# Two row blocks of table 1 made ahead of the first addition, and the edge lists of target blocks 5 to 7 made earlier

## The chip, the cores and the metric

The kernel runs on one core of one Trainium2 chip. A core has five engines that run side by side and meet only through semaphores: PE (matrix products; weight loads are shown apart as PEld), DVE (vector work), ACT (activations and copies), POOL (here: it issues the gathers) and SP (here: it issues nearly all other transfers). Sixteen DMA engines move the data of all queues. The metric is the device time of one execution in microseconds (us), the median of several runs; lower is better.

## The reference

For each of 16 batches b, with 1024 nodes and 256 features, the layer gates each edge (u, v) of a sparse adjacency matrix (well under 1% of the entries, and the diagonal):

```
pre_u = h_t @ W1[:256]            # per source node u
pre_v = h_t @ W1[256:]            # per target node v
hidden = relu(pre_u[:, :, None, :] + pre_v[:, None, :, :] + b1)
S = sigmoid(hidden @ W2 + b2)
a_t = einsum('buv,bud->bvd', S * A_a, h_t)
m_t = einsum('uv,bud->bvd', A_m, h_t) * h_t
z_t = beta1 * h_t + beta2 * (a_t @ Wa + ba) + beta3 * (m_t @ Wm + bm)
```

Both A_a and A_m are `adj`. Only pairs with an edge matter, so the kernel works on lists of edges.

## The kernel before, in words

**Tiles.** The batches form 4 groups of 4. For each group g there is a table in DRAM (`table[g]`) with one row of 8 KB per source node: 4 KB of pre_u and 4 KB of h for the 4 batches. The 1024 nodes form 8 blocks of 128. A *row block* (g, nt) is the part of table g that belongs to source block nt; it is made from hT (the transposed h of that block, 0.5 MB, in pieces of 512 bytes) by `rows`: two halves, each a product with `w_u` on PE (`half_product`, L411), a copy from PSUM by ACT into `tab` and a write into the table by SP. The h half of the row is copied from DRAM to DRAM by SP (`copy_h`, L405).

**Lists.** For each target block vt, `lists(vt)` makes the list of its edges from one 0.5 MB piece of `adj` (`key`, loaded by SP at L238): DVE finds the nonzero places (L245, L254 to L300), ACT turns them into marks (`made`, L305 to L307), PE permutes them (L315), ACT copies the outcome (`few`, L309, and L, L319) and DVE finishes with indices (L323 to L344). Lists 0 to 3 are made ahead of the main loop; lists 4 to 7 are generators whose pieces are put between the loop's work by `fill` and `piece_of`. What a generator yields says when its next piece may come: after "load" 8 steps, after "wait" 2, after "slot" or "step" 1.

**Main loop.** The work is 32 blocks (one group and one target block each) of T = 10 steps, 320 steps n. In a step POOL gathers 128 table rows for 128 edges into one of 8 slots (`fetched`, L513, about 1 MB); PE expands the target side onto the edges (`expand`, L622: pc from the marks and X); DVE adds it (`add`, L652) and gates with relu and W2 (`gate`, four operations at L659); ACT makes the sigmoid and the weights (`left`, L662, L666); PE sums into the targets (`aggregate`, L675). A slot is free for the next gather once PE has summed from it, so up to 8 gathers run ahead; the first 8 need no freed slot. At each block's end PE transposes sums (L697) and multiplies with Wa and Wm (L746), and SP writes the result (L753). `halves(k)` makes X, the target side of block k (L415, L411 with `w_v`, L472, and `low` at L474 on DVE). The last blocks go without `low`.

**Order.** No scheduler sorts this: each engine and each queue runs its instructions in the order in which the program is written. Blocks come as group 0 with vt 0 to 5, group 1 with vt 0 to 5, group 0 with 6 and 7, group 1 with 6 and 7, then groups 2 and 3. So table 1 must be whole when the gathers of block 6 (step 60) are issued, some 8 steps earlier, and list 6 is needed for block 12. Ahead of the loop a `script` of 14 strings sets the order of the start by letters: "r" is half a row block of table 0, a digit is a piece of that list, "f" issues the first 8 gathers, "w" six warming products on PE whose result nobody reads (`warm`, L553), "h" a piece of X, "k" loads the hT of row block (1,6), "m" makes the first mark and "s" scales the bias. In the loop `made_rows(n)` makes half a row block of table 1 in the steps that `plan` lists, after loading its hT some steps earlier, when a place for it is free. There are 2 places of hT beside the 8 of group 0, which come free one after another; 3 more (`MORE`) come when all lists are done, at step `LISTS`.

Of the kernel before, what the change touches and what calls it, by code (L numbers as in the profile page):

```python
# [17 lines left out]
def kernel(  # L18
# [217 lines left out]
    def lists(vt):  # L236
# [68 lines left out]
        nc.scalar.activation(mark, slot, AF.Abs, bias=span[:, 1:2])  # L305
        nc.scalar.activation(mark, mark, AF.Sign, bias=span[:, 0:1], scale=-1.0)
        nc.scalar.activation(mark, mark, AF.Relu)  # L307
        yield "step"
        nc.scalar.copy(few, mark)  # L309
        for w in range(NW):  # L310
            for h in range(2):
# [186 lines left out]

    BS = NG * NT
    EVS = 3  # L500
    ROOM, MORE, LISTS, AHEAD = 10, 3, 110, 14
    BEHIND = (5, 6, 7, 8)
    APART, minus = 24, []

# [33 lines left out]
    for i in range(COPIES):  # L538
        copy_h(turn[i], nc.sync)

    script = ("r r 0 0", "r r 1 0 0", "r r 1", "r 0 0", "r r 1", "0 2 r 1", "0 0 r r", "1 2 r 1", "v r r 2", "r 1 3",
              "h 2 1 1", "h 2 2 3", "f 2 2 2 k w h h h", "m 3 w 3 3 3 s")
    begun_rows = {}
    marks, pcs, accs, evs, hbs, LTs, lefts = {}, {}, {}, {}, {}, {}, {}

# [14 lines left out]
        nc.vector.scalar_tensor_tensor(bias_c, bias_c, be3, ba_c, ALU.mult, ALU.add)  # L560
        hT_free.append(spare_)

    m = 0
    piece = None
    parts = halves(0)
    for t, turns_ in enumerate(script):
        step = t - 100
        do(step)
        for c in turns_.split():
            if c == "r":  # L570
                k = turn[m % NT]
                if m < NT:
                    begun_rows[k] = rows(k, tabs[m])
                    next(begun_rows[k])
                go(begun_rows[k], step)
                if m > NT and m - NT + COPIES <= NT:
                    copy_h(turn[m - NT + COPIES - 1], nc.sync)
                m += 1
            elif c == "h":
                go(parts, step)  # L580
            elif c == "v":
                fetch_val(3)
                spread(b1_p, b1_b)
                next(parts)
            elif c == "f":
                for n in range(NF):
                    fetch(n)
                    if n > 2:
                        fetch_val(1)
                bias = load_rows(bm, D, "bias", nc.sync, spare[:, 1])  # L590
                ba_b = load_rows(ba, D, "ba_b", nc.sync, spare[:, 2])
                bias_c, ba_c = fixed([P, DC], "bias_c"), fixed([P, DC], "ba_c")
                nc.sync.dma_start(bias_c, bm.rearrange("(c p) -> p c", p=P))
                nc.sync.dma_start(ba_c, ba.rearrange("(c p) -> p c", p=P))
                be1 = load_rows(beta1, 1, "be1", nc.sync)
                be2 = load_rows(beta2, 1, "be2", nc.sync)
                be3 = load_rows(beta3, 1, "be3", nc.sync)
            elif c == "k":
                load_hT(turn[NT])
            elif c == "s":  # L600
                scale_bias()
            elif c == "m":
                load_mark(0)
            elif c == "w":
                warm(6)
            else:
                next(made[int(c)], None)
# [28 lines left out]
    def piece_of(r, n):  # L636
# [2 lines left out]
        if said is None:  # L639
            running.remove(r)  # L640
        else:
            r[1:] = said not in ("slot", "step"), n + {"load": 8, "wait": 2, "slot": 1, "step": 1}.get(said, 0)

    def fill(n, gap=True):
        for r in running:
# [154 lines left out]


    advance = {0: (3,), 2: (3,), 4: (3,)}
    start_list = dict(zip((7, 14, 44, 82), range(EARLY, NT)))
    at, pending = {}, []

    def plan(blocks, ns):
# [2 lines left out]
            pending.append((pieces[0], k))  # L809
            at.update((n, k) for n in pieces)  # L810

    plan(turn[NT:], ((4, 6), (9, 11), (13, 18), (19, 21), (23, 28), (29, 31), (33, 38), (39, 41)))
    for g, first in ((2, 60), (3, 140)):
        plan([(g, vt) for vt in range(NT)], ((first + 9 + 10 * i, first + 14 + 10 * i) for i in range(NT)))
    pending.extend((order.index(k) * T - T + 1, k) for k in again)
    pending.sort()
    ending = parts = piece = last = None

# [71 lines left out]
    for n in range(total - 3):  # L890
# [17 lines left out]
        if n == 0:  # L908
            for i in advance[0]:
                next(made[i], None)  # L910
            load_hT(turn[NT + 1])
            next(made[EARLY])
            w_a, w_m = load_weights(Wa, "w_a", nc.sync), load_weights(Wm, "w_m", nc.sync)
            after(10, scale_weights)
        if n == total - 6:
            hbs[BS - 1] = next(t for t in hT_free if t in flat).rearrange("p b c n -> p b (c n)")
# [174 lines left out]
```

## Time and profile before

| | us |
|---|---|
| median of 3 runs | 1029.48 |
| lowest and highest | 1023.5, 1036.24 |
| the profiled execution | 1026.43 |
| its span, first to last instruction | 1024.6 |
| mean granted clock of PE in it | 0.984 |

The page gives, for the whole span, each engine's busy time and then, in 40 slices of 25.6 us, its busy share in tenths. A row of the timeline has the start, the time, the engine and line, output and input, and in brackets how long the engine was idle before it and what ended that. SPq and POOLq rows are issues of transfers: the time there is that of the issue, not of the transfer. Rows of the DMA queues have packets, MB and the share of 16 engines' time; q0 carries the gathers that POOL issues, q1 what SP issues. A row of the windows has busy time of PE, PEld, DVE, ACT and POOL, then PE's clock, the DMA share and GB/s.

### The profile page before, as it was taken

What the parts mean: (1) busy time and instruction counts of PE and PEld (TensorE: products, weight loads), DVE (VectorE), ACT (ScalarE), POOL (GpSimd) and SP (SyncE); (2) the same over time, 40 slices, a digit from 0 to 9 for tenths busy, and PEclk for the clock granted to TensorE, in tenths of its full rate; (3) what the DMA queues carried; (4) which work ended last, traced back from release to release, by engine and by line L of the source; (5) the groups of instructions that cost most, each with busy time, mean ns of one, the idle gap of its engine ahead of it and who ended that gap; (6) DMA issues with size and microseconds to landing.
All of it is one profiled execution on the core that took longest, in us unless ns stands there. A gap on an engine that the chain in (4) does not pass through costs nothing.

```text
span 1024.6 us, 21644 instructions
## 1 busy us (share of the span) xinstructions
PE 957.0 (93%) x6408; PEld 696.9 (68%) x6408; DVE 948.3 (93%) x3302; ACT 889.0 (87%) x2754; POOL 438.2 (43%) x441
## 2 busy tenths in 40 slices
PE   7877989998899999999999999999999999999996
PEld 5744766665566766776677777777777666677663
DVE  7588969879998999998999999999999999999994
ACT  3666978978898999888999999999999999999984
POOL 3166656555337332563343333434333434444430
PEclk9988999999999999999999999999999999999998
DMA  9899999999899999999999999999999999999992
GB/s 329 300 356 383 376 340 322 351 364 343 301 342 343 396 412 387 343 365 381 411 414 411 411 406 405 412 393 414 383 413 394 383 375 365 365 370 368 377 369 70
DMA packets 128702, 375.00 MB, mean 366 GB/s; under 512 B 17616, under 2 KB 83152, under 8 KB 92368
## 3 DMA queue, kind: packets, MB, share of 16 engines
q0 software_dynamic: 48640, 296.70, 74.3%
q1 hardware_dynamic: 79312, 76.30, 22.4%
q8 instruction: 53, 0.87, 0.3%
q10 hardware_dynamic: 624, 0.52, 0.2%
q14 instruction: 73, 0.60, 0.2%
HBM read 377.53 MB, written 50.33 MB: 418 GB/s over the span
## 4 chain that ended last, share of the span: by engine, by line
PE 56%; DVE 23%; ACT 8%; issue 8%; DMA 3%; POOL 1%; another core or an unknown queue 0%; POOLq 0%; DVEq 0%
PE misc L411 16%; DVE fetched L659 11%; PE misc L746 11%; PE pc L622 10%; PE acc L675 9%; DVE fetched L652 8%; PE misc L697 4%; DMA fetched<-table,uidx 3%; ACT left L666 2%; PE misc L730 1%; DVE LT L714 1%; PE misc L415 1%; ACT ev L683 1%; ACT X L906 1%; POOL fetched L513 1%
## 5 line engine op out<-in xcount | busy, mean ns | idle before, releaser
L513 POOL DMA_INDIRECT fetched<-table,uidx x320 | 342.7, 1071 | 501.3 <-PE acc L675 353.8
L659 DVE SCALAR_TENSOR_TENSOR fetched<-fetched,w_b 128x256 f32<-128x256 f32 x1280 | 472.3, 416 | 0.0
L652 DVE TENSOR_TENSOR fetched<-fetched,pc 128x1024 f32<-128x1024 f32 x320 | 387.6, 1211 | 28.9 <-PE pc L622 10.2
L666 ACT ACTIVATE left<-left,gt 128x16 f32<-128x16 f32 x1280 | 285.8, 299 | 0.0
L622 PE MATMUL pc<-X,mark 128*128 128x512 f32 x640 | 229.8, 451 | 20.7 <-DVE fetched L652 11.9
L675 PE MATMUL acc<-fetched,left 128*32 128x256 f32 x2560 | 183.6, 388 | 4.6 <-ACT ev L683 3.1
L622 PEld LDWEIGHTS pc<-X,mark 128*128 128x128 f32 x640 | 105.0, 189 | 109.8 <-issue 59.3
L675 PEld LDWEIGHTS acc<-fetched,left 128*32 128x32 f32 x2560 | 71.8, 109 | 81.9 <-issue 23.2
L662 ACT ACTIVATE gt<-sc,b_b 128x4 f32<-128x4 f32 x320 | 96.8, 303 | 30.4 <-DVE fetched L659 22.0
L746 PE MATMUL misc<-w_a,LT 128*128 128x256 f32 x496 | 117.4, 379 | 0.7 <-ACT LT L424 0.7
L746 PE MATMUL misc<-w_m,LT 128*128 128x256 f32 x496 | 117.3, 379 | 0.0
L746 PEld LDWEIGHTS misc<-w_a,LT 128*128 128x128 f32 x496 | 93.6, 189 | 15.6 <-ACT LT L424 1.5
L630 ACT ACTIVATE left<-onehot,val 128x32 f32<-128x32 bf16 x320 | 100.1, 313 | 0.0
L411 PE MATMUL misc<-w_u,wide 128*128 128x256 f32 x384 | 92.0, 388 | 8.0 <-DMA w_u<-in_W_dram 7.3
L353 POOL DMA_INDIRECT val<-in_adjT_dram,vidx x80 | 85.0, 1063 | 33.8 <-issue 22.8
L659 DVE DVE_READ_ACCUMULATOR fetched<-fetched,w_b 128x1 f32 x1280 | 99.0, 77 | 0.0
L683 ACT COPY ev<-acc 128x512 f32<-128x512 f32 x160 | 92.3, 577 | 6.8 <-PE acc L675 2.3
L746 PEld LDWEIGHTS misc<-w_m,LT 128*128 128x128 f32 x496 | 89.5, 190 | 9.8
L697 PE MATMUL misc<-ident,ev 128*128 128x128 f32 x642 | 83.9, 275 | 11.7 <-ACT ev L683 5.8
L411 PE MATMUL misc<-w_v,wide 128*128 128x256 f32 x368 | 91.5, 394 | 0.0
L697 PEld LDWEIGHTS misc<-ident,ev 128*128 128x128 f32 x642 | 74.5, 142 | 22.4 <-ACT ev L683 6.6
L411 PEld LDWEIGHTS misc<-w_u,wide 128*128 128x128 f32 x384 | 73.6, 194 | 21.1 <-DMA w_u<-in_W_dram 7.3
(160 smaller groups left out, 980.2 us busy)
## 6 DMA issues: line engine op xcount, KB each, us to landing
table<-in_x_dram SPq DMA_DIRECT2D x32, 512.0 KB
out_dram<-z SPq DMA_DIRECT2D x62, 256.0 KB
table<-tab SPq DMA_DIRECT2D x48, 256.0 KB
wide<-in_xT_dram SPq DMA_DIRECT2D x18, 512.0 KB
fetched<-table,uidx POOLq DMA_INDIRECT x320
hT<-in_xT_dram SPq DMA_DIRECT2D x10, 512.0 KB
wide<-in_xT_dram SPq DMA_DIRECT2D x4, 1024.0 KB
table<-fetched SPq DMA_DIRECT2D x8, 512.0 KB
```

Source lines behind the costliest of these rows:

```text
L411: nc.tensor.matmul(p[:, bb * D:(bb + 1) * D], hT[:, 2 * h + bb, i, :], wt[:, i, :], start=(i == 0 and not begun), stop=(i == DC - 1), skip ...
L513: nc.gpsimd.indirect_dma_start(out=fetched[at_slot[n]], out_offset=None, in_=table[g], in_offset=bass.IndirectOffsetOnAxis(ap=uidx[:, vt * ...
L622: nc.tensor.matmul(pcs[n][:, c], marks[n // TW][:, j * P:(j + 1) * P], cuts[k][w][:, c], start=True, stop=True)
L630: nc.scalar.activation(lefts[n][:, 1::GB, :], onehot[:, vt * NW + w, j, :].unsqueeze(1).to_broadcast([P, GB // 2, V]), AF.Copy, scale=val[ ...
L652: nc.vector.tensor_tensor(t, t, pcs.pop(n), ALU.add)
L659: nc.vector.scalar_tensor_tensor(t[:, b, :], t[:, b, :], 0.0, w2_b, ALU.max, ALU.mult, accum_out=sc[:, b:b + 1])
L662: nc.scalar.activation(gt, sc, AF.Sigmoid, bias=b2_b)
L666: nc.scalar.activation(lefts[n][:, 2 * b, :], lefts[n][:, 1 + b // 2 * GB, :], AF.Copy, scale=gt[:, b:b + 1])
L675: nc.tensor.matmul(accs[i][b * 2 * V:(b + 1) * 2 * V, r, :], left[:, 2 * b - b % 2:2 * b - b % 2 + 2].rearrange("p k v -> p (k v)"), f[:, ...
L683: nc.scalar.copy(evs[i], accs.pop(i))
L697: nc.tensor.matmul(pt[:, :, FROM[j]:FROM[j] + V], evs[i][:, r, c * P:(c + 1) * P], ident, is_transpose=True, start=(j == of[0]), stop=True ...
L746: nc.tensor.matmul(pz[:, bb * D:(bb + 1) * D], LT[:, 2 * h + bb, i if bb else 1 - i, c, :], wt[:, c, :], start=(i == 1 and bb == 0 and c = ...
```

## The change

- In the script, "k" now comes right behind "f" and loads two hT places, of (1,6) and (1,7). The second group of six warming products is gone. A new letter "x" makes half a row block; four of them stand at the end of the last two strings, so (1,6) and (1,7) are made ahead of the first addition.
- Their `copy_h` moves to step 0, behind the loads of list 4's key and of w_a and w_m. The load of hT (1,7) in step 0 is gone.
- The other six row blocks of table 1 are made in steps 8 and 9, 13 and 18, 19 and 23, 28 and 29, 33 and 38, 39 and 43 (before: eight row blocks in steps 4 to 41).
- Lists 6 and 7 start in steps 27 and 40 instead of 44 and 82, and a list waits 5 steps for its load instead of 8. `LISTS` goes from 110 to 70.
- After the three ACT operations of `made` a list now pauses 2 steps ("pause") instead of 1 ("step").
- The hT of the row blocks that are needed a second time is asked for 9 steps sooner.

```
-        yield "step"
+        yield "pause"
         nc.scalar.copy(few, mark)
...
-    ROOM, MORE, LISTS, AHEAD = 10, 3, 110, 14
+    ROOM, MORE, LISTS, AHEAD = 10, 3, 70, 14
...
-              "h 2 1 1", "h 2 2 3", "f 2 2 2 k w h h h", "m 3 w 3 3 3 s")
+              "h 2 1 1", "h 2 2 3", "f k 2 2 2 w h h h x", "m 3 x 3 3 3 s x x")
...
             elif c == "k":
-                load_hT(turn[NT])
+                for k in turn[NT:NT + 2]:
+                    load_hT(k)
+                sooner = [rows(k) for k in turn[NT:NT + 2]]
+            elif c == "x":
+                if x_made % 2 == 0:
+                    next(sooner[x_made // 2])
+                go(sooner[x_made // 2], step)
+                x_made += 1
...
-            r[1:] = said not in ("slot", "step"), n + {"load": 8, "wait": 2, "slot": 1, "step": 1}.get(said, 0)
+            r[1:] = (said not in ("slot", "step", "pause"),
+                     n + {"load": 5, "wait": 2, "slot": 1, "step": 1, "pause": 2}.get(said, 0))
...
-    start_list = dict(zip((7, 14, 44, 82), range(EARLY, NT)))
+    start_list = dict(zip((7, 14, 27, 40), range(EARLY, NT)))
...
-    plan(turn[NT:], ((4, 6), (9, 11), (13, 18), (19, 21), (23, 28), (29, 31), (33, 38), (39, 41)))
+    plan(turn[NT + 2:], ((8, 9), (13, 18), (19, 23), (28, 29), (33, 38), (39, 43)))
...
-    pending.extend((order.index(k) * T - T + 1, k) for k in again)
+    pending.extend((order.index(k) * T - 2 * T, k) for k in again)
...
-            load_hT(turn[NT + 1])
             next(made[EARLY])
             w_a, w_m = load_weights(Wa, "w_a", nc.sync), load_weights(Wm, "w_m", nc.sync)
+            for i in turn[NT:NT + 2]:
+                copy_h(i, nc.sync)
```

Line numbers behind the script grow by up to 8 (`expand` L622 becomes L629, `add` L652 becomes L660, `aggregate` L675 becomes L683).

On PE, this stands between the last list-2 product and the first product for block 1, before (hT_203 is the load of (1,6); `wide` holds the hT of group 0, and in the changed kernel that of (1,7) in a part that has come free):

```order
L315 MATMUL pc<-RR,made 128x56 x5
L553 MATMUL acc<-b_p,unit 128x512 x12
L279 MATMUL misc<-ahead,before 128x5
L280 MATMUL misc<-start__98,ident 128x5
L622 MATMUL pc<-X,mark 128x512 x6
L415 MATMUL misc<-b_p,unit 128x512
```

And in the changed kernel:

```order
L315 MATMUL pc<-RR,made 128x56 x5
L553 MATMUL acc<-b_p,unit 128x512 x6
L411 MATMUL misc<-w_u,hT_203 128x256 x8
L279 MATMUL misc<-ahead,before 128x5
L280 MATMUL misc<-start__98,ident 128x5
L411 MATMUL misc<-w_u,wide 128x256 x8
L629 MATMUL pc<-X,mark 128x512 x6
L415 MATMUL misc<-b_p,unit 128x512
```

Half the warming products went, the products of (1,6) stand ahead of list 3's first products (L279), and those of (1,7) ahead of the first expansion, which the first addition waits for.

On SP's queue, the same place as one piece of the difference (`whose<-few` are the marks of lists 2 and 3):

```order
 L91 DMA be_596<-in_beta_dram 128x1
-L312 DMA whose<-few 64x640 x4
 L400 DMA hT_203<-in_xT_dram 128x8x128
-L312 DMA whose<-few 64x640 x4
-L400 DMA wide<-in_xT_dram 128x8x128
+L400 DMA wide<-in_xT_dram 128x8x128
+L312 DMA whose<-few 64x640 x4
+L439 DMA table_61<-tab_640 128x512
+L439 DMA table_61<-tab_663 128x512
+L439 DMA table_61<-tab_694 128x512
+L439 DMA table_61<-tab_701 128x512
+L312 DMA whose<-few 64x640 x4
```

Both hT loads moved ahead of the marks of list 2, and the four table writes of (1,6) and (1,7) stand ahead of the marks of list 3, behind which list 4's key is loaded.

On PE in block 2, around list 4's products (L315), before:

```order
L675 MATMUL acc<-fetched_183,left 32x256 x4
L622 MATMUL pc<-X,mark 128x512 x2
L411 MATMUL misc<-w_u,hT_204 128x256 x4
L622 MATMUL pc<-X,mark 128x512 x2
L315 MATMUL misc<-RR,made 128x56 x5
L415 MATMUL misc<-b_p,unit 128x512
L411 MATMUL misc<-w_v,wide 128x256 x4
L675 MATMUL acc<-fetched_184,left 32x256 x4
L675 MATMUL acc<-fetched_185,left 32x256 x4
L622 MATMUL pc<-X,mark 128x512 x2
```

And in the changed kernel:

```order
L683 MATMUL acc<-fetched_183,left 32x256 x4
L629 MATMUL pc<-X,mark 128x512 x2
L411 MATMUL misc<-w_u,hT_203 128x256 x4
L629 MATMUL pc<-X,mark 128x512 x2
L415 MATMUL misc<-b_p,unit 128x512
L411 MATMUL misc<-w_v,wide 128x256 x4
L683 MATMUL acc<-fetched_184,left 32x256 x4
L683 MATMUL acc<-fetched_185,left 32x256 x4
L629 MATMUL pc<-X,mark 128x512 x2
L315 MATMUL misc<-RR,made 128x56 x5
```

List 4's products stand one step later, behind the products for the next X and two sums.

2 lines of the change are left out of this document (1 added, 1 removed).

## The prediction

> **What bounds the kernel now.** I read the page first (busy shares and slices), then the additions of the loop by window, then the start in order of time, then the DMA queues by window.
>
> ```profile
> PE 957.0 (93%) x6408; PEld 696.9 (68%) x6408; DVE 948.3 (93%) x3302; ACT 889.0 (87%) x2754; POOL 438.2 (43%) x441
> ...
> PE   7877989998899999999999999999999999999996
> ...
> DVE  7588969879998999998999999999999999999994
> ...
> DMA  9899999999899999999999999999999999999992
> ```
>
> DVE and PE are both full from about slice 13 on; only the first third has holes. There are 320 steps, and each begins with one addition on DVE (L652). The next rows are that line in three windows (number of additions, then the first and last start):
>
> ```profile
> L652 DVE TENSOR_TENSOR fetched<-fetched,pc x120: 1202/1212/1222, 95.5 to 486.6; 128x1024 f32<-128x1024 f32 x120
> L652 DVE TENSOR_TENSOR fetched<-fetched,pc x20: 1202/1206/1221, 362.6 to 422.8; 128x1024 f32<-128x1024 f32 x20
> L652 DVE TENSOR_TENSOR fetched<-fetched,pc x80: 1203/1210/1222, 489.2 to 709.1; 128x1024 f32<-128x1024 f32 x80
> ```
>
> Blocks 13 to 20 (third row) take (709.1-489.2)/79 = 2.78 us a step. That is DVE without a gap: the chain of waits has these two pieces one after the other in every quiet step, 2.51 us together, and the rest is the product with h and the subtraction of `low`.
>
> ```profile
> 272.31 1.13 DVE fetched L652
> 273.44 1.38 DVE fetched L659 x8
> ```
>
> Blocks 1 to 12 (first row) take (486.6-95.5)/119 = 3.29 us a step, 394 us for 120 steps. Blocks 9 and 10 (second row), which hold all of list 7 and nothing else unusual, take (422.8-362.6)/19 = 3.17, so one list costs 20 x (3.17-2.78) = 7.8 us when DVE is full. Four lists (4 to 7) are 31 us. So 120 x 2.78 + 31 = 365 us would be DVE's own time in blocks 1 to 12, and 394 - 365 = 29 us are waits. That, and the start, are all that this change can touch.
>
> **The start.** Ahead of the first addition stand these rows of the timeline:
>
> ```profile
> 48.97 1.42 SPq L91 DMA_DIRECT2D be<-in_beta_dram  x3
> 50.70 4.42 PE L553 MATMUL acc<-b_p,unit 128*128 128x512 f32 x12
> 51.59 0.99 POOL L513 DMA_INDIRECT fetched<-table,uidx  x1 [17.08 <-DMA ba_c<-in_ba_dram]
> 53.04 0.59 SPq L400 DMA_DIRECT2D hT<-in_xT_dram  x1
> 60.37 1.22 DVE L652 TENSOR_TENSOR fetched<-fetched,pc 128x1024 f32<-128x1024 f32 x1
> 61.64 1.22 PE L622 MATMUL pc<-X,mark 128*128 128x512 f32 x2 [3.86 <-issue]
> 63.09 3.62 PE L411 MATMUL misc<-w_v,wide 128*128 128x256 f32 x8
> 70.41 1.89 PE L411 MATMUL misc<-w_v,wide 128*128 128x256 f32 x8
> 70.59 1.23 POOL L513 DMA_INDIRECT fetched<-table,uidx  x1 [0.64 <-issue]
> 72.12 0.53 SPq L400 DMA_DIRECT2D wide<-in_xT_dram  x1
> 72.69 2.67 SPq L238 DMA_DIRECT2D key<-in_adjT_dram  x1
> 80.22 0.58 ACT L424 COPY tab<-misc 128x512 f32<-128x512 f32 x1 [2.27 <-PE misc L411]
> 91.74 0.69 DVE L245 SCALAR_TENSOR_TENSOR key<-key,ukey 128x512 f32<-128x512 f32 x1 [4.72 <-DMA key<-in_adjT_dram]
> ```
>
> The warming products (L553) need no load. The hT load of row block (1,6) is issued at 53.04 and has until step 4 to land, so its latency shows nowhere. In the changed kernel PE multiplies (1,6) and (1,7) before the first expansion, so both loads stand between the gathers' start and the first addition. What a load costs there the queues show; these are the page's row for all gathers, then the windows 54.2 to 57, 57 to 58, 58 to 72 (with its packet sizes) and 78 to 80 us, each queue with its packets, MB and share:
>
> ```profile
> q0 software_dynamic: 48640, 296.70, 74.3%
> ...
> q1 hardware_dynamic: 165, 0.09, 10.1%
> ...
> q0 software_dynamic: 32, 0.24, 62.4%
> q1 hardware_dynamic: 322, 0.16, 54.6%
> ...
> DMA packets 1492, 5.65 MB, mean 403 GB/s; under 512 B 219, under 2 KB 843, under 8 KB 843
> q0 software_dynamic: 853, 5.30, 94.2%
> q1 hardware_dynamic: 637, 0.32, 8.0%
> ...
> q1 hardware_dynamic: 807, 0.43, 88.8%
> ```
>
> From 58 to 72 there are 843-219 = 624 packets of 512 B (hT's rows of 128 floats, q1) and 1492-843 = 649 of 8 KB (gathered rows, q0): one for one. So beside running gathers q1 gets 0.32/14 = 0.023 MB/us; with q0 nearly empty (last row) it gets 0.43/2 = 0.22. A load queued beside gathers crawls. The list's key shows it from outside: 0.5 MB issued at 72.69 behind an hT load, and DVE waits for it until 91.74.
>
> **The change, part by part.**
>
> *Removed:* six of twelve warming products, 4.42/2 = 2.2 us of PE that nothing waited for: 0.
>
> *Moved ahead: two loads, four half products, four copies, four writes.* SP issues the loads right behind the `be` loads, at 50.4 and 51.0 instead of 53.0 and 72.1. Gathers 0 to 7 need no free slot, so they run whatever PE does. Each is 296.70/320 = 0.93 MB; at 5.30/14 = 0.38 MB/us that is 2.45 us, and eight of them from 54 with the hole at 57 end near 74 to 75. The two loads are 1.05 MB. About 0.2 MB passes before the gathers start (53 to 54 us at 0.22), 0.09 until 57, 0.16 in the hole, so 0.45 by 58; then 16.5 us at 0.023 give 0.38; what is left, 0.22 MB, goes at 0.22 once the gathers have run out. So (1,6) lands near 62 and (1,7) near 76, 77 with its completion. PE then needs 16 passes for (1,7). It has idled, and after its idle time at 61.64 eight passes took 3.62 us instead of 1.89, so 3.62 + 1.89 = 5.5, and the expansion 1.2: first addition at 83.7 instead of 60.4, **+23.3 us**. Bounds: at the full rate of the window 58 to 72 (403 GB/s) both loads are there by 56, and PE has only 4 x 1.89 - 2.2 us more to do than now, most of it behind the list's own wait: +4. From above, two loads at the key's 19 us each would land at 89 and give +35, but gathers that have run out can't slow them so long: +27. I take 23 since the packet rows are this very load at this very time. On ACT four copies of 0.6 us stand before the first `left`; in that wait they cost nothing, and without it 1.8 us. List 3 and the bias wait behind (1,6) on PE and are done by 72, hidden under (1,7). SP's four table writes wait for those copies, and the marks of list 3, the key of list 4, w_a, w_m and two row copies queue behind them.
>
> The Trainium skill, page "DMA: Bandwidth & Descriptors", section Specifications, gives 512 B as the smallest transfer that still reaches line rate. By it the loads would be there by 56 and this term +4 instead of +23. The rows say that this holds for q1 alone (0.22 MB/us) and not beside 8 KB packets, so I sum with the rows.
>
> *Block 0.* It loses two row blocks' products (4 x 1.89 = 7.6 us of PE) and probably the 4.72 us wait for list 4's key, which no longer queues behind an hT load. It gains one row block in steps 8 and 9 whose load is issued in step 2 only, behind the key, w_a, w_m and two row copies: 2.6 MB in the ten us or so before step 8, where the full q1 rate gives 2.2. PE will wait there some 5 to 8 us. I set the block to its present 35 us: **0**, between -6 and +8.
>
> *Blocks 1 to 12*, 29 us of waits. The chain in block 2 runs through list 4's marks on ACT into PE:
>
> ```profile
> 134.14 0.72 ACT made L305
> 134.89 0.83 ACT made L306
> 135.75 0.75 ACT made L307
> 136.54 1.32 PE misc L315 x10
> ...
> DVE fetched L652 <- PE acc L675: 4.9, 1, 4.9
> DVE fetched L652 <- PE acc L675: 4.1, 2, 2.2
> DVE fetched L652 <- PE pc L622: 2.4, 1, 2.4
> ```
>
> The last three are DVE's waits in blocks 2, 4 and 7. The pause puts the products of L315 a step later, behind other PE work, so PE no longer waits for `made`: 4.9 for list 4 and little for the others, -6. Blocks 1 to 4 have about 1.5 row blocks each instead of 2, which relieves PE in block 4's wait: -4. Lists 6 and 7 leave blocks where DVE is full (16 us for both) for blocks 3 to 5, where it waits some of the time: -4, the rest only changes place. Three more hT places from step 70 rather than 110: -2 of block 7's wait. Against it, the keys of lists 5 to 7 are read 5 or 6 steps after their load is issued instead of 8 and more, 16 us where the key above took 19: +2. Together **-14**, between -4 (the pause alone, less the keys' waits) and -22 (most of the 29).
>
> Sum: 1026.43 + 23.3 + 0 - 14 = 1035.7, **1036 us**, against the profiled execution's own 1026.43; that lies 3 us below the median of the runs shown (1029.48), which the range has to hold too.
>
> **Rivals.** *B, the loads are in time.* If q1 gets its bytes before the gathers take the engines (the skill's rule above), the start costs +4, block 0 keeps -5 (key and rows) and blocks 1 to 12 their -14: 1011 us. For it: SP's loads are queued 1 us before POOL's first gather, and 0.16 MB passed in one hole. Against it: 624 to 649.
>
> *C, the late start is never repaid (slower).* DMA, not PE or DVE, may hold blocks 1 to 12; then the time in which the queues stand empty, from 76 until a slot is free again (gather 8 is issued at 70.59, 10 us after the first addition), is lost.
>
> ```profile
> 95.46:128.70 33.24, 32.54 (x206) 24.33 (x204) 31.39 (x122) 28.92 (x88) 21.82 (x22) 0.97 1.05 376
> 128.70:170.36 41.66, 36.45 (x222) 26.00 (x222) 33.20 (x123) 32.44 (x94) 25.89 (x25) 0.96 0.95 326
> 572.00:600.00 28.00, 28.00 (x197) 21.13 (x196) 27.73 (x94) 26.71 (x85) 10.30 (x10) 1.00 1.03 412
> ```
>
> For it: a DMA share (the column before the last) of 1.05 in block 1, as in full block 16 (last row). Against it: 0.95 in block 2, and 376 and 326 GB/s where 412 are possible. Price: +23 and about +2 for the keys, nothing back: 1052. It decides if the share stays at 1.03 or more in blocks 1 to 5 while a step still takes over 3.2 us.
>
> *D, only the first load is late*: (1,6) lands at 62 as above and (1,7) right behind it, if the gathers leave more holes with PE waiting than now. Two times 3.8 us of products, the list's two and the expansion then end near 71: +10 and -14, 1022 us. Against it: the window 58 to 72 has no hole (94.2%).
>
> **Chances.** A (mine) 0.58, its own range 1026 to 1049; B 0.16; C 0.16; D 0.10. A difference under about 2% (1009 to 1050 around the median) can't be told from no change here. Faster by over 2% needs B and more recovered than I count: 0.05. Slower by over 2%: most of C and the top of A, 0.14. The rest, 0.81, is within 2%. The range from 1011 to 1052 leaves out half of B and half of C, some 0.16.
>
> **What the new profile would show.** The first addition near 84 and PE idle for over 10 us between the products of hT and of `wide`, ended by a load: A. First addition before 66: B. q0's share falls to near nothing between 76 and 90. No wait of DVE for the first key over 2 us. PE waits at step 8 or 9 for an hT load. `made` to L315 no longer on the chain in block 2. 120 additions of blocks 1 to 12 in 380 us (A) or 394 (C). The sum is wrong if q1 does not share packet for packet, or if the 29 us are held by DMA.

## The result, and the profile after

| | before | changed |
|---|---|---|
| median, us | 1028.74 (17 runs) | 1033.04 (17 runs) |
| lowest and highest | 1020.22, 1036.24 | 1027.61, 1044.78 |
| the profiled execution, its span | 1026.43, 1024.6 | 1031.42, 1029.6 |

The ratio is 1.0061, with a 95% interval of 1.0039 to 1.0082: within 2%, and on the slow side of no change. Here and below a ratio is taken over the fast runs of both kernels, so it is not quite that of the two medians (here 1.0042). The prediction was 1036 (1011 to 1052). The time is near it, the way there is not, as the terms below show.

The page of the changed kernel, busy time over the whole span and in 40 slices:

```profile
PE 955.5 (93%) x6402; PEld 700.0 (68%) x6402; DVE 947.3 (92%) x3302; ACT 889.3 (86%) x2754; POOL 440.9 (43%) x441
...
DVE  7568698899999999997999799999999999999994
...
```

Busy sums are those of before within 3.1 us, so hardly any work was saved or added. The holes moved: DVE has deeper ones in slices 3 and 5 (6 tenths instead of 8 and 9), none any more in slice 6 (9 instead of 6), and lower shares in slices 19 (7 instead of 8) and 23 (7 instead of 9), in a part that was nearly full before. The starts of the additions (L652, now L660) at the borders of blocks give the balance of the two profiled spans:

| stretch | before, us | changed, us | difference |
|---|---|---|---|
| start to first addition | 60.37 | 68.19 | +7.8 |
| block 0 | 35.09 | 28.77 | -6.3 |
| block 1 | 33.24 | 44.70 | +11.5 |
| blocks 2 to 6 | 174.62 | 173.89 | -0.7 |
| blocks 7 to 11 | 154.01 | 140.00 | -14.0 |
| blocks 12 to 16 | 142.72 | 150.24 | +7.5 |
| the rest | 424.55 | 423.81 | -0.7 |
| span | 1024.6 | 1029.6 | +5.0 |

**The start.** Rows of the timeline of the changed kernel (start, time, engine and line; in brackets the idle time before it and what ended that):

```profile
50.40 0.43 SPq L400 DMA_DIRECT2D hT<-in_xT_dram  x1
50.93 0.53 SPq L400 DMA_DIRECT2D wide<-in_xT_dram  x1
51.42 0.99 POOL L513 DMA_INDIRECT fetched<-table,uidx  x1 [17.12 <-DMA ba_c<-in_ba_dram]
57.64 6.16 PE L411 MATMUL misc<-w_u,hT 128*128 128x256 f32 x16 [3.81 <-DMA hT<-in_xT_dram]
63.99 3.70 PE L411 MATMUL misc<-w_u,wide 128*128 128x256 f32 x16
68.19 2.35 DVE L660 TENSOR_TENSOR fetched<-fetched,pc 128x1024 f32<-128x1024 f32 x2 [0.44 <-PE pc L629]
```

PE waited 3.81 us for the first load. The second was in place before PE asked for it: the products of `wide` follow without a wait. The DMA queues say why. First the window 54.2 to 57 us, then 57 to 58, then 58 to 72 (sizes of the packets, then a queue's packets, MB and share of 16 engines' time):

```profile
DMA packets 1649, 0.80 MB, mean 285 GB/s; under 512 B 92, under 2 KB 1649, under 8 KB 1649
q1 hardware_dynamic: 1649, 0.80, 99.5%
...
q1 hardware_dynamic: 452, 0.23, 90.6%
q0 software_dynamic: 12, 0.10, 30.5%
...
DMA packets 1388, 5.59 MB, mean 399 GB/s; under 512 B 217, under 2 KB 522, under 8 KB 799
q0 software_dynamic: 704, 4.81, 85.7%
```

In the first window q0 has no packet at all, although POOL had issued gathers from 51.42 on. The loads went nearly whole (0.80 + 0.23 MB of 1.05), and the gathers began to move only near 57.5, where before they began at 53.7. PE then worked slowly (6.16 us for 16 passes, 3.70 for the next 16), and so the first addition came at 68.19. PE's granted clock, the column before the last two, goes with that: 0.50 in the first of the two stretches below, 1.00 in the second. In the kernel before it was 0.99 from 55.1 to 60 us, behind all twelve warming products; whether the six that are gone would have kept it up here, no run shows.

```profile
57.64:60.50 2.86, 2.86 (x7) 2.32 (x8) 0.00 (x0) 0.00 (x0) 1.99 (x2) 0.50 1.08 402
63.99:67.69 3.70, 3.70 (x19) 3.29 (x19) 3.24 (x15) 2.93 (x5) 0.99 (x1) 1.00 1.03 403
```

**Blocks 0 and 1.** The load of row block (1,0) and what waits for it, in the same timeline:

```profile
84.03 8.01 SPq L400 DMA_DIRECT2D wide<-in_xT_dram  x1
106.58 3.78 PE L411 MATMUL misc<-w_u,wide 128*128 128x256 f32 x8 [12.15 <-DMA wide<-in_xT_dram]
111.93 0.99 POOL L513 DMA_INDIRECT fetched<-table,uidx  x1 [11.18 <-PE acc L683]
112.25 1.22 DVE L660 TENSOR_TENSOR fetched<-fetched,pc 128x1024 f32<-128x1024 f32 x1 [12.64 <-PE pc L629]
```

PE stands 12.15 us in front of (1,0)'s products, and with it DVE (12.64), since the next expansion is behind them on PE, and POOL (11.18), since no slot comes free. Block 1's row of the windows shows it in every column: PE 34 of 44.7 us, and only 305 GB/s on the DMA engines, because the gathers stood still.

```profile
96.96:141.66 44.70, 34.02 (x206) 25.71 (x206) 31.39 (x120) 29.61 (x93) 21.76 (x22) 0.85 0.90 305
```

**Blocks 2 to 16.** The windows of five blocks each, of before and then of the changed kernel (length; busy time of PE, PEld, DVE, ACT, POOL; PE's clock, DMA share, GB/s):

```profile
128.70:303.32 174.62, 157.78 (x1030) 111.56 (x1029) 153.34 (x546) 145.85 (x440) 87.78 (x82) 0.99 0.95 338
303.32:457.33 154.01, 147.73 (x988) 107.24 (x984) 145.20 (x504) 137.89 (x428) 76.24 (x70) 0.99 1.00 372
457.33:600.05 142.72, 140.19 (x960) 104.16 (x953) 138.43 (x470) 133.12 (x421) 53.03 (x51) 1.00 1.03 406
```

```profile
141.66:315.55 173.89, 158.30 (x1026) 111.83 (x1027) 159.11 (x583) 149.76 (x446) 107.91 (x98) 0.99 0.95 336
315.55:455.55 140.00, 139.00 (x949) 104.07 (x948) 138.49 (x467) 132.94 (x420) 58.95 (x55) 1.00 1.02 393
455.55:605.79 150.24, 143.41 (x972) 106.28 (x971) 138.96 (x472) 134.13 (x421) 53.00 (x51) 0.99 1.03 400
```

Read DVE's column first: list 7 moved some 6 us of it from blocks 7 to 11 (145.20 to 138.49) into blocks 2 to 6 (153.34 to 159.11), where it fitted into waits, since these got no longer. Blocks 7 to 11 came down nearly to DVE's own time: of their 14.0 us, 6.7 are list work of DVE that went elsewhere, and about 6 are DVE's waits for PE and ACT, which fell from 8.6 us to 2.5. Then read the last column: blocks 12 to 16 have the same 139 us of DVE work as before and take 7.5 us more, with the DMA engines at 1.03. Multiplying length by rate, blocks 7 to 16 moved 57.3 + 57.9 = 115.2 MB before and 55.0 + 60.1 = 115.1 MB now. The bytes are the same, and no row of five blocks in this text shows more than 406 GB/s.

### The profile page after: what moved, and what is told of

Its sections match the earlier page's. It is cut to its first block, busy times and chain, and to the rows that moved or that the text cites. A ratio compares the mean times of both kernels' runs of the same rounds, so it can differ in the third digit from the quotient of the medians.

```text
span 1029.6 us, 21627 instructions
## 1 busy us (share of the span) xinstructions
PE 955.5 (93%) x6402; PEld 700.0 (68%) x6402; DVE 947.3 (92%) x3302; ACT 889.3 (86%) x2754; POOL 440.9 (43%) x441
## 4 chain that ended last, share of the span: by engine, by line
PE 53%; DVE 23%; DMA 8%; ACT 7%; issue 6%; SPq 1%; POOL 1%; POOLq 0%; DVEq 0%; another core or an unknown queue 0%
PE misc L411 14%; DVE fetched L667 12%; PE misc L754 11%; PE pc L629 11%; PE acc L683 9%; DVE fetched L660 9%; PE misc L705 4%; DMA wide<-in_xT_dram 2%; DMA fetched<-table,uidx 2%; ACT left L674 2%; PE misc L738 1%; DVE LT L722 1%; DMA table<-in_x_dram 1%; DMA fetched<-in_adjT_dram 1%; PE misc L415 1%
## 5 line engine op out<-in xcount | busy, mean ns | idle before, releaser
L660 DVE TENSOR_TENSOR fetched<-fetched,pc 128x1024 f32<-128x1024 f32 x320 | 387.3, 1211 | 38.9 <-PE pc L629 16.8
L629 PE MATMUL pc<-X,mark 128*128 128x512 f32 x640 | 226.7, 448 | 17.3 <-DVE fetched L660 14.3
L683 PE MATMUL acc<-fetched,left 128*32 128x256 f32 x2560 | 188.1, 389 | 9.0 <-issue 4.2
L629 PEld LDWEIGHTS pc<-X,mark 128*128 128x128 f32 x640 | 105.5, 189 | 103.5 <-issue 53.8
L683 PEld LDWEIGHTS acc<-fetched,left 128*32 128x32 f32 x2560 | 74.5, 109 | 87.3 <-issue 26.4
L353 POOL DMA_INDIRECT val<-in_adjT_dram,vidx x80 | 89.4, 1117 | 35.4 <-issue 21.5
L411 PE MATMUL misc<-w_v,wide 128*128 128x256 f32 x352 | 84.4, 383 | 0.0
```

The costliest lines, as they stand in the source:

```text
L411: nc.tensor.matmul(p[:, bb * D:(bb + 1) * D], hT[:, 2 * h + bb, i, :], wt[:, i, :], start=(i == 0 and not begun), stop=(i == DC - 1), skip ...
L629: nc.tensor.matmul(pcs[n][:, c], marks[n // TW][:, j * P:(j + 1) * P], cuts[k][w][:, c], start=True, stop=True)
L660: nc.vector.tensor_tensor(t, t, pcs.pop(n), ALU.add)
L683: nc.tensor.matmul(accs[i][b * 2 * V:(b + 1) * 2 * V, r, :], left[:, 2 * b - b % 2:2 * b - b % 2 + 2].rearrange("p k v -> p (k v)"), f[:, ...
```

## The experiments

Each group of kernels ran on one chip, beside the kernel before, which took 1025.4 us there with the first four, 1012.9 with the next four, 1012.5 with the third group and 1025.9 with the last. Times are compared inside a group; between groups only ratios to before are. On the two quicker chips blocks 2 to 6 of the variants take 161 to 163 us instead of 172 to 177; why is not settled. The kernel before and the changed kernel were profiled apart from these groups, so a length compared with theirs may be compared across chips.

### The two halves

The first kernel is before with the loop half of the change only (lists, their waits, `LISTS`, the second hT loads), the second is the changed kernel with that half put back.

```
e1, against before:
-        yield "step"
+        yield "pause"
-    ROOM, MORE, LISTS, AHEAD = 10, 3, 110, 14
+    ROOM, MORE, LISTS, AHEAD = 10, 3, 70, 14
-    start_list = dict(zip((7, 14, 44, 82), range(EARLY, NT)))
+    start_list = dict(zip((7, 14, 27, 40), range(EARLY, NT)))
...
e2, against the changed kernel: the same lines, - and + exchanged
```

> The kernel before with the loop half of the change only: pause, 5 steps after a load, list starts 7, 14, 27, 40, LISTS 70, the second hT loads 9 steps sooner. The start, the row blocks' steps and the warming products stay as before. Theory 1 (the two halves of the change add up; the lists bring the 13 us that blocks 2 to 12 gained, and one of LISTS or the sooner second loads brings the new 5 us stall between blocks 15 and 16): first addition at 60.4, blocks 2 to 12 shorter by about 13, the stall of block 15 present, time about 1028.7 - 13.4 + 6 = 1021 (1016 to 1024). Theory 2 (the relief came from the one and a half row blocks that left blocks 1 to 4, not from the lists): blocks 2 to 12 shorter by 2 to 6 only, time 1027 to 1033.

> The changed kernel with the loop half put back (step instead of pause, 8 steps after a load, list starts 7, 14, 44, 82, LISTS 110, second hT loads as before), so only the start and the row blocks' steps are changed. Theory 1 (halves add up): first addition at 68, block 0 about 29, PE and DVE wait some 11 us in step 10, nothing or a few us back in blocks 2 to 12, no stall in block 15; time about 1028.7 + 7.8 - 6.3 + 11.5 = 1042 (1037 to 1044). Theory 2 (the row blocks' absence gives the relief): blocks 2 to 12 shorter by 8 to 13, time 1028 to 1034.

e1: 1021.37 us, ratio 0.9966 (0.9931 to 1.0001). e2: 1039.77 us, ratio 1.0132 (1.0062 to 1.0202). The windows of blocks 2 to 6, 7 to 11 and 12 to 16, of e1 and then of e2:

```profile
126.62:302.60 175.98, 161.72 (x1047) 116.03 (x1045) 159.30 (x584) 151.04 (x448) 105.23 (x97) 0.97 0.97 343
302.60:441.78 139.18, 138.04 (x945) 103.63 (x945) 138.59 (x465) 132.93 (x420) 57.96 (x55) 1.00 1.02 396
441.78:590.28 148.50, 143.65 (x984) 106.91 (x986) 138.75 (x470) 134.02 (x421) 53.35 (x51) 0.99 1.02 400
```

```profile
144.24:316.08 171.84, 155.67 (x1015) 110.44 (x1013) 153.31 (x546) 145.22 (x438) 85.08 (x81) 0.97 0.93 330
316.08:469.11 153.03, 145.36 (x968) 105.38 (x961) 144.92 (x504) 136.71 (x425) 75.62 (x70) 1.00 1.01 379
469.11:612.01 142.90, 140.68 (x975) 105.36 (x974) 138.86 (x472) 134.21 (x424) 53.56 (x51) 1.00 1.02 401
```

Against before the lists alone do -14.8 in blocks 7 to 11, +5.8 in 12 to 16 and +1.4 in 2 to 6; the start alone does -2.8 in blocks 2 to 6 and next to nothing behind them. So the gain belongs to the loop half, and what is given back in blocks 12 to 16 comes with it. Within that half e1 doesn't tell the list starts from `LISTS` and from the shorter wait for a load. The start half is a loss of 1.3%: block 1 took 47.28 us in e2, much as in the changed kernel. The first theory held for e2. For e1 the time lies in its range only because this chip is quicker: by ratio the lists alone gained 3.5 us, where 1016 to 1024 against 1028.7 meant 5 to 13. In e1 it also missed the place: the additional waits stood in block 12 and, 5.6 us, in block 21, not in block 15.

### Who is queued first

```
-              ... "f k 2 2 2 w h h h x", ...
+              ... "f 2 2 2 k w h h h x", ...
```

> The changed kernel with one letter moved: the two hT loads are issued behind the marks of list 2, where the kernel before issued its one, so behind the first gather instead of ahead of it. Theory 1 (what was queued first went first; a load queued beside running gathers shares packet for packet with them, as in the kernel before): the first load lands past 65 and the second past 72, first addition at 80 to 86, time 1041 to 1049. Theory 2 (the loads go first wherever they are issued, or PE's products and not the loads set the start): first addition at 68 to 71, time 1033 to 1036.

1044.08 us, ratio 1.0139 (1.0070 to 1.0209). The same two loads were issued at 54.30 and 54.99 instead of 50.40 and 50.93, now behind the first two gathers. Its timeline, and then its queues from 58 to 72 us:

```profile
76.36 6.46 PE L411 MATMUL misc<-w_u,hT 128*128 128x256 f32 x16 [23.40 <-DMA hT<-in_xT_dram]
87.23 2.35 DVE L660 TENSOR_TENSOR fetched<-fetched,pc 128x1024 f32<-128x1024 f32 x2 [0.46 <-PE pc L629]
```

```profile
DMA packets 1912, 5.59 MB, mean 399 GB/s; under 512 B 214, under 2 KB 1299, under 8 KB 1299
...
q0 software_dynamic: 789, 5.02, 89.3%
q1 hardware_dynamic: 1122, 0.57, 14.0%
```

Four microseconds later in the queue cost 19 us at the first addition (87.23 against 68.19). q1 got 0.57 MB in 14 us: the crawl on which the prediction counted is real, for loads that are queued behind gathers. The first theory stands; 87.23 is 1 us past its range. Of those 19 us the whole time shows about 8, by the two ratios: a late start is in part made up later.

### The wait in step 10

```
         if n == 0:
...
+            load_hT(turn[NT + 2])
             next(made[EARLY])
```

> The changed kernel with the hT load of row block (1,0) issued in step 0, ahead of list 4's key, w_a, w_m and the two row copies, instead of in step 2 behind them. Theory 1 (the wait of 12.6 us in step 10 comes from that load's late place in SP's queue): the wait falls under 3 us, the key's grows by at most 3, time 1033 - 10 = 1023 (1020 to 1026). Theory 2 (the DMA engines hold block 0 and 1, whichever transfer comes first): the wait turns up elsewhere in blocks 0 and 1, at the key or at a gather, first addition of block 2 within 3 us of 141.7, time 1030 to 1035.

1020.81 us, ratio 0.9942 (0.9908 to 0.9976), the lowest ratio of all kernels here, with an interval below 1, though well within 2%. SP's issues and the products of (1,0) in its timeline, and then the windows of blocks 0 and 1:

```profile
78.59 0.57 SPq L400 DMA_DIRECT2D wide<-in_xT_dram  x1
79.20 2.90 SPq L238 DMA_DIRECT2D key<-in_adjT_dram  x1
...
95.18 1.89 PE L411 MATMUL misc<-w_u,wide 128*128 128x256 f32 x8
```

```profile
69.17:99.50 30.33, 25.47 (x136) 15.09 (x135) 28.43 (x92) 19.76 (x65) 19.51 (x19) 0.83 1.04 393
99.50:130.73 31.23, 28.16 (x175) 20.58 (x175) 31.23 (x120) 28.19 (x88) 20.87 (x20) 1.00 1.05 395
```

The products run at 95.18 instead of 106.58 and without a wait for the load; block 1 falls from 44.70 to 31.23 and block 0 rises by 1.6. That is the first theory: by ratio 12 us less than the changed kernel, where it said 10 (7 to 13).

### The second loads, the pause, and both loads sooner

Three single edits of the changed kernel and one pair, on one chip:

```
e5
-    pending.extend((order.index(k) * T - 2 * T, k) for k in again)
+    pending.extend((order.index(k) * T - T + 1, k) for k in again)
e6
-        yield "pause"
+        yield "step"
e7
-              ... "f k 2 2 2 w h h h x", ...
+              ... "k f 2 2 2 w h h h x", ...
e8: the edit of e4 and that of e5
```

> The changed kernel with one piece undone: the hT loads of the row blocks that are needed a second time are asked for as late as before (9 steps later). Theory 1 (those sooner loads push the last table writes of group 2 back in SP's queue, and that is the stall of 4.6 us between blocks 15 and 16): stall gone, blocks 13 to 16 shorter by 5 to 6, time about 1033 - 5.5 = 1027.5. Theory 2 (the DMA engines are full from block 9 on, 1.03 of their time in both kernels, and the stall is where the backlog shows, whichever load is asked for first): the stall stays or moves, time 1031 to 1035.

> The changed kernel with one piece undone: one step instead of two between the marks of a list (three operations on ACT) and the products that use them. Theory 1 (the pause takes PE's wait for the marks off the path, as the prediction has it with 6 us): blocks 2 to 5 longer by 4 to 7 in sum, the rows of the marks and of L315 back on the chain, time 1037 to 1040. Theory 2 (the marks are ready in time anyway now that fewer row blocks stand there): within 2 us of the changed kernel.

> The changed kernel with the two hT loads issued one letter sooner, ahead of the bias and beta loads and of the first gathers. Theory 1 (the loads set the first addition, and what is queued first goes first): they land 2 to 3 us sooner, first addition at 65 to 66.5, time 1030 to 1031.5. Theory 2 (they only take the place of the bias and beta loads, or of the last loads of the start, and the products of list 3 or the gathers are late instead): first addition at 68 or later, time 1033 or more.

> The changed kernel with (1,0)'s hT load in step 0 ahead of the key, w_a, w_m and the row copies, and with the second hT loads as late as before: the two repairs together. If both stalls are what the reading of the trace says: 1020.8 - 5.5 = 1015 (1013 to 1018). If the stall of block 15 is the DMA engines' backlog: 1019 to 1023.

| kernel | us | ratio to before | first addition | block 2 begins | block 17 begins |
|---|---|---|---|---|---|
| e5 | 1018.38 | 1.0065 (1.0035 to 1.0096) | 68.68 | 141.63 | 590.31 |
| e6 | 1021.60 | 1.0071 (1.0042 to 1.0100) | 68.65 | 141.07 | 591.79 |
| e7 | 1015.22 | 1.0033 (1.0008 to 1.0057) | 64.13 | 139.80 | 589.61 |
| e8 | 1013.69 | 1.0015 (0.9982 to 1.0047) | 69.43 | 133.98 | 588.43 |

*e5.* The additions of steps 159 and 160 are 2.5 us apart, as in e8, against 4.9 in e6 and 8.0 in e7 on the same chip: without the sooner loads no trace has that stall (2.5 us in before, e2, e5 and e8). They don't make it alone: e3, e10 and e11 have them too, and 2.5 us there. What else it takes is not shown. And a single wait, between steps 127 and 128, is 7.9 us here, and blocks 12 to 16 take 148.66 us against 149.71 in e7. The ratio is that of the changed kernel: locally the first theory, in time the second.

*e6.* What the weight loads of L315 and its products waited for in blocks 2 to 6 of e6 (in total, times, longest); in e5 neither waits for the marks there:

```profile
PEld misc L315 <- ACT made L307: 6.1, 3, 2.8
...
PE misc L315 <- ACT made L307: 4.8, 3, 2.4
```

The two rows show the same three waits. Without the pause PE waits 4.8 us for the marks again, yet blocks 2 to 11 take 162.96 + 138.59 = 301.55 us, against 161.55 + 138.47 = 300.02 in e5 and 300.09 in e7. The pause is worth 1.5 us there; the rest of that wait had cost nobody anything. The second theory holds.

*e7 and e8.* The first addition came 4.1 us sooner in e7 and block 2 only 1.9 us: PE reached (1,0) earlier and waited longer for the same load (13.54 us against 12.15). By ratio e7 takes some 3 us less than the changed kernel, as its first theory said. e8 began block 2 some 7.7 us before e5 and block 17 only 1.9 us before it. What it lost stands mostly in one row of block 12, where PE waits for an hT load and DVE, for 8.43 us, for the expansion behind it:

```profile
446.41 3.41 PE L411 MATMUL misc<-w_v,wide 128*128 128x256 f32 x8 [6.74 <-DMA wide<-in_xT_dram]
```

The absolute time of e8 lies in the first theory's range only because this chip is quicker; by ratio neither number is met.

### Bytes or stalls

```
e9
-                out[b:b + 2, vt * P:(vt + 1) * P, :].rearrange("b p d -> p b d"), o))
+                out[b:b + 2, vt * P:vt * P + 16, :].rearrange("b p d -> p b d"), o[:16]))
e10
-        if n == 120:
+        if n == 72:
             nc.vector.tensor_tensor(rest, rest, taken, ALU.subtract)
             nc.gpsimd.partition_all_reduce(longest, rest, P, bass_isa.ReduceOp.max)
e11: the edits of e4 and of e7
e12: the edits of e9 and of e10
```

> The changed kernel, but SP writes only 16 of the 128 rows of each result z (the last two target blocks apart): every instruction and wait stays, 0.46 MB per block less goes through the DMA engines. Theory 1 (from block 7 on the DMA engines are full at 400 to 406 GB/s, all kernels have moved 219 to 220 MB by block 17, and what the lists save in blocks 7 to 11 comes back as waits for gathers in blocks 12 to 16): blocks 12 to 16 take 138 to 143 us together instead of 150, no wait of DVE for a gather over 2 us in steps 120 to 169, time 8 to 12 us below the changed kernel. Theory 2 (two local stalls, of POOL's reduction near step 125 and of a late table write near step 159, whatever the DMA engines carry): blocks 12 to 16 take 147 to 151 us, the gather's waits stay.

> The changed kernel with the one reduction over partitions on POOL (which keeps POOL from issuing gathers for some 9 us) at step 72 instead of 120. Theory 1 (the DMA engines hold blocks 7 to 16): the wait near step 127 goes, and as much comes back elsewhere; blocks 7 to 16 together within 3 us of 290, time 1031 to 1035 on the chip of the changed kernel, ratio to before 1.003 to 1.008. Theory 2 (POOL's hole by itself holds block 12): blocks 12 to 16 shorter by 4 to 5, blocks 7 to 11 longer by at most 1, ratio to before 1.000 to 1.003.

> The changed kernel with both repairs of the start: the two hT loads one letter sooner, and (1,0)'s load in step 0 ahead of the key. Theory (both gains add up: 12 us of step 10's wait, 3 to 4 us of the first addition): first addition at 64 to 66, block 2 begins 4 to 6 us sooner than with the second repair alone (130.7), ratio to before 0.990 (0.987 to 0.995). Rival (what the start gains is lost again to the DMA engines in blocks 7 to 16): block 2 begins sooner, block 17 does not; ratio 0.994 to 1.001.

> The kernel with 16 of 128 rows of z written, and POOL's reduction at step 72 besides. Theory (the 150 us of blocks 12 to 16 in the changed kernel are DVE's own 139 us, 4 us behind POOL's reduction and 7 us for which the DMA engines were full): without the bytes the reduction's hole is filled up again where it now stands, blocks 12 to 16 take 138.5 to 140 us and DVE waits for no gather over 1 us there; blocks 7 to 11 at most 141. Rival (the 4 us come back somewhere in blocks 12 to 16 as they did with all bytes written): 142 to 144 us.

What the reduction of e10 does on POOL shows in the timeline, of before and then of the changed kernel: 8 to 9 us without a gather.

```profile
474.79 0.59 POOL L937 PARTITION_ALL_REDUCE longest<-rest  x1 [8.80 <-ACT gt L662]
```

```profile
473.99 0.39 POOL L946 PARTITION_ALL_REDUCE longest<-rest  x1 [8.43 <-ACT gt L670]
```

DVE's waits in blocks 12 to 16 (in total, times, longest), of before, the changed kernel, e9, and e10 (two rows):

```profile
DVE fetched L652 <- DMA fetched<-table,uidx: 4.2, 2, 3.9
```

```profile
DVE fetched L660 <- DMA fetched<-table,uidx: 9.7, 4, 4.6
```

```profile
DVE fetched L660 <- DMA fetched<-table,uidx: 3.9, 1, 3.9
```

```profile
DVE fetched L660 <- PE pc L629: 8.4, 6, 4.1
DVE fetched L660 <- DMA fetched<-table,uidx: 0.2, 1, 0.2
```

And the windows of blocks 7 to 11 and 12 to 16, of e9 and then of e12:

```profile
302.81:441.40 138.59, 138.59 (x961) 104.06 (x951) 138.41 (x469) 133.33 (x421) 58.47 (x56) 1.00 1.03 395
441.40:584.44 143.04, 141.14 (x972) 105.31 (x971) 138.61 (x471) 133.63 (x421) 53.74 (x51) 1.00 1.00 392
```

```profile
318.93:463.91 144.98, 139.97 (x946) 103.81 (x945) 138.50 (x469) 132.85 (x420) 59.34 (x56) 1.00 0.97 372
463.91:603.69 139.78, 139.78 (x972) 105.33 (x971) 139.09 (x468) 134.24 (x421) 52.00 (x50) 1.00 1.03 403
```

*e9* (1010.41 us, ratio 1.0004, 0.9980 to 1.0027). With 0.46 MB per block less, blocks 12 to 16 take 143.04 us, and DVE waits there once, 3.9 us, just as before: that one is POOL's hole (e10 and e12, which move it, have no such wait). So each theory was right about a part: 4 us are local and stood in the kernel before too; the other 5 to 7 (148.02 in e10, 150.24 in the changed kernel) went with the bytes. In time e9 misses: by ratio it takes about 6 us less than the changed kernel, not 8 to 12.

*e10* (1019.44 us, ratio 1.0107, 1.0061 to 1.0154). With all bytes written, moving the hole gains next to nothing: the wait behind step 127 is gone, blocks 12 to 16 take 148.02 us all the same, with waits for PE now around steps 122 and 132 (PE itself waits for hT loads there, 2.22 us at 448 us and 3.78 us at 480). Blocks 7 to 16 together take 139.65 + 148.02 = 287.7 us, against 288.3 in e7 on a chip of the same speed. The first theory holds for these blocks; the ratio lies above the range given, though its interval reaches into it.

*e12* (1029.06 us, ratio 1.0036, 0.9984 to 1.0089). With fewer bytes and the hole elsewhere, blocks 12 to 16 come down to 139.78 us, DVE's own time, without a wait. But blocks 7 to 11 then hold 5.3 us of waits for gathers, 4.0 of them at the end of block 7, behind the hole, and where 141 us were expected for five blocks, 145 came. That part of the expectation missed; the chip is one of the slower ones, and the two causes are not told apart.

*e11* (1010.46 us, ratio 0.9981, 0.9946 to 1.0016). Here the start's two repairs do not add up. Its timeline:

```profile
73.61 0.52 SPq L400 DMA_DIRECT2D wide<-in_xT_dram  x1
...
97.78 3.78 PE L411 MATMUL misc<-w_u,wide 128*128 128x256 f32 x8 [7.95 <-DMA wide<-in_xT_dram]
100.82 0.70 DVE L245 SCALAR_TENSOR_TENSOR key<-key,ukey 128x512 f32<-128x512 f32 x1 [12.30 <-DMA key<-in_adjT_dram]
```

The first addition came at 62.58, yet (1,0)'s load, issued 5 us before e4's, arrived 2.6 us after the moment at which e4 already used it, and the key held DVE for 12.30 us. An earlier first addition frees slots earlier, and the next gathers then stand beside the load. From 72 to 96 us the queues of the changed kernel, of e4 and of e11 carried 7.13, 6.63 and 7.58 MB on q0 and 2.30, 2.67 and 1.69 MB on q1, at 394, 388 and 387 GB/s in all: one sum, shared out differently. The rival has the ratio right, but not the place: the gain is lost in block 0 already, and block 2 began at 135.69, 5 us later than in e4.

## Why the prediction came out as it did

The forecast of 1036 and the measured 1033.04 agree because errors of opposite signs met. Its own terms:

- **First addition, predicted +23.3, measured +7.8.** This is the step that failed: "About 0.2 MB passes before the gathers start ... then 16.5 us at 0.023 give 0.38". The rows behind it (624 to 649 packets) showed a load that had been queued behind gathers, and the text put that price on loads queued ahead of them. It even named the fact that decides, under rival B ("SP's loads are queued 1 us before POOL's first gather"), and weighed it as the lesser one. The 0.2 MB did not pass early either: nearly nothing moved on the engines from 51 to 53.8 us (1 GB/s), and then q1 had them to itself. e3 and the changed kernel show both sides: behind the first gathers, 87.23, near the predicted 83.7; ahead of them, 68.19. Rival B's price for loads in time was +4, and e7, where PE finds both loads there, has +3.8. What the changed kernel has beyond that goes with PE's wait of 3.81 us for the first load and its first products at the low clock shown above (6.16 us against 4.38 in e7). Rival D's picture, only the first load late and the second right behind it, comes nearest to this start, though (1,6) came near 57.6 and not at 62, and not through holes in the gathers.
- **Block 0, predicted 0, measured -6.3, with +11.5 in block 1.** The mechanism was right, both ways, though the wait fell into block 1: the key's wait went, and PE waited for (1,0)'s load behind the key, w_a, w_m and the row copies. The size was not: 5 to 8 us predicted, 12.15 measured. The sum of bytes against time was made for a full q1; in fact q1 shared 72 to 96 us with the gathers. e4 shows that it was SP's order.
- **Blocks 1 to 12, predicted -14, measured -1.9.** Without the 11.5 us of block 1, blocks 2 to 12 gained 13.4 us, but not from the parts that were added up. The pause, put at 6, is worth 1.5 (e6). The row blocks, put at 4, brought about 3 (e2). The lists out of DVE-full blocks, put at 4 since "the rest only changes place", brought, with the rest of the loop half, 13 (e1: -14.8 and +1.4): in blocks 2 to 6 they went into waits nearly free of charge. The text's own price for lists in full blocks, 16 us for two, comes near this by luck: DVE's list work in blocks 7 to 11 was that of list 7 alone, 6.7 us, and nearly as much went in waits for PE and ACT, which the sum did not have there.
- **Blocks 13 to 16, not in the sum at all: +6.** That is the mechanism of rival C, DMA as the bound, at a place where C did not look. C asked about blocks 1 to 5; there the changed kernel has a share of 0.95 and 336 GB/s. In blocks 7 to 16 both kernels move the same 115 MB, and once DVE's list work was out of the way the DMA engines held back blocks 12 to 16, as e9 shows, with POOL's hole beside them as before. Where the waits stand changes (4.8 of the 6 us are the stall between steps 159 and 160, which e3, e5 and e10 don't have), but with the lists moved and all bytes written blocks 12 to 16 take 146 to 154 us in every run, against 142.7 and 142.9 in before and e2.

Of the signs promised, the first addition lay at 68.19, between those for A (84) and B (66), nearer to B, and PE did not idle between the products of hT and of `wide`. q0's share did not fall to nothing from 76 to 90 (93.7% up to 80 us, 74.9% after it): the gathers had begun later, and with the first addition at 68 the next slots came free sooner than reckoned. No key held DVE, PE waited for an hT load, and `made` no longer held L315: all as said. Blocks 1 to 12 took 391.9 us, near the 394 of C, though for another reason.

The Trainium skill (page "DMA: Bandwidth & Descriptors", Specifications), weighed in the prediction with its 512 bytes for line rate, would, by the prediction's reckoning, have had both loads there by 56; PE got the first at 57.64, after a wait, and the second without one. The trace agrees only in part: alone on the engines from 54.2 to 57, the 512-byte packets moved at 285 GB/s, a mean that takes in their start (278 to 351 in the slices behind it), against 399 from 58 to 72 with 8 KB rows among them.

The best version here is the changed kernel with one load moved (e4, ratio 0.9942); the loop half alone (e1, 0.9966), on the same chip, is as good within the intervals. On the quicker chips that load was moved only together with another edit (e8, 1.0015, and e11, 0.9981), so e4's gain stands on one chip. What early row blocks could add to the lists is therefore not shown to be more than nothing.

## What to carry to other kernels

A rate read from two queues that run together holds for the order in which their transfers were queued; before you price a load that is moved, see on which side of the big transfers it will stand, and count everything on its queue ahead of it. When work leaves a full engine, ask at once what the next bound of that stretch is: here 115 MB at 400 to 406 GB/s take 284 to 288 us, so of the 296.7 us of blocks 7 to 16 no more than 9 to 13 could go, and 6.5 went. A wait that goes from the chain is worth what the engine behind it can use, not its length: 4.8 us of waiting were worth 1.5.

## What the runs showed of the hardware

Two hT loads queued 0.5 to 1 us ahead of the first gather went through nearly whole, with q0 at no packet for 2.8 us (54.2 to 57); queued behind two gathers, they took until 76.36. The Trainium skill (page "DMA: Bandwidth & Descriptors", Queues, rings and completion order) says that a DMA engine takes turns between its queues packet by packet. By that the gathers, issued from 51.42 on, would have had their turns in that window; the trace shows none there. The counts beside running gathers (58 to 72 us) differ from run to run: 624 small to 649 large in the kernel before, 1085 to 613 in e3. They don't test the page, whose packet can hold several of the pieces that the profile counts. What decides it is left open.

One reduction over partitions, 0.4 to 0.6 us long on POOL, came with 8.4 to 8.8 us in which POOL issued nothing (6.3 in e10, at step 72). And the same kernel before took 1012.5 to 1028.7 us on different chips, a difference as large as most effects in this text.
